# Third layer of a four-layer image model: the gates of each tap spread over the channels by transfers from DRAM, the products taken from SBUF over two chunks at a time, one copy of the values

## The chip, the cores and the metric

The kernel runs on one core of a Trainium2 chip. The metric is the device time of one execution in microseconds (us). Engine names are those of the profile: PE is the matmul engine and PEld its weight loads, DVE is VectorE, ACT is ScalarE, POOL is GpSimd, SP is the engine whose queue issues the transfers. All arithmetic spoken of here is f32.

## The reference, cut to what matters

Four layers work on an image batch of 4 x 64 x 64 pixels with 128 channels. The first two are selective scans in four directions, the fourth is a 7x7 neighbourhood attention. Only the third layer is changed. For each pixel and each of its nine neighbours (a tap) it computes two small perceptrons on the pixel and the neighbour, makes a gate of them, and averages the neighbours' values by these gates:

```
norm   = ln(tokens)                                   # 128 channels
edge   = [center, neigh, center - neigh, rel_pos]     # per pixel and tap, 9 taps
drive  = gelu(edge @ d_w1 + d_b1) @ d_w2 + d_b2       # one number per pixel and tap
resist = gelu(edge @ r_w1 + r_b1) @ r_w2 + r_b2
gate   = sigmoid(clip(lam * drive / (softplus(resist) + gamma + eps)) + bias)
values = neigh @ v_w + v_b                            # 128 channels
message = sum_taps(gate * values) / sum_taps(gate)
out    = ln(tokens + message @ o_w + o_b)
```

The gate is one number per pixel and tap, the values have 128 channels, so each gate has to reach all 128 channels before it can be multiplied.

## The kernel before

Channels lie on the 128 partitions, pixels on the free axis. An image of 4096 pixels is 8 chunks of T = 512 pixels (8 rows of 64), and the third layer works by halves of an image: four chunks. `layer2` runs over four images `b` and two halves `s`, eight halves in all, and writes out by hand the order in which work is issued; each engine takes its instructions in that order, and semaphores do the rest.

One half has two parts. `edges(b, s, side)` makes 18 steps (two perceptrons, nine taps each). A step adds the neighbours' projections (`near`, in SBUF) to the centre's (`cen`, in PSUM) with two DVE additions of 128x1024 (L1277), applies Gelu in two ACT instructions (L1282), and sums over channels with four small matmuls into `out` (L1253). Five buffers hold `hid`. Between the steps it issues pieces of the list `side`, evenly spread over the 18 steps. Then comes the fill: `gates` turns `out` into the gates `g` in five pieces (`one` to `five`, mostly DVE), and a few pieces of the next half are put between them. In `g` row 32*j + t holds tap t of chunk j.

The pieces of `side` belong to neighbouring halves:

- `finish` of the half before the last: per chunk a scaling on POOL (L1405), an ACT instruction, and a store to DRAM (L1410).
- `gather` of the last half: 18 gate pieces and then four output pieces per chunk. A gate piece is one tap of one pair of chunks: PE multiplies the rows of `g` with a 0/1 matrix `pick` so that the gate appears on all 128 partitions in PSUM (L1361), DVE multiplies it with the shifted values (L1367), one 128x512 instruction for each chunk, and POOL adds the product to `acc` (L1371), one for each chunk. The output pieces load the tokens (`xo`), apply the output weights, and take the variance (L1382 to L1388, L1209).
- `statistics` of the next image: per chunk a load on SP (`xs`, two buffers, L1191), a centring matmul (L1195) with an ACT copy, a square on POOL (L1200), a variance matmul (L1209) with an ACT copy.
- `project`: per chunk a scaling on POOL (L1219), then three matmuls (L1223) with an ACT write each (L1229): two into `near`, the third into the values `vals`, which are kept twice, for even and odd images.

The matmuls of all these pieces share two PSUM banks (`bank()`, tag mm). Every transfer is issued by SP in program order, so a transfer that waits holds the ones behind it. After the last half `layer2` runs `finish` and `gather` once more with nothing beside them; this is called the tail below. Before the first half it prepares the first image (the start-up).

The order of one gather, whose two loops the change turns round, is

```
out = [begin] + [lambda t=t, pair=pair: gate(t, pair) for pair in range(2) for t in range(NB)]
```

Of the kernel before, what the change touches and what calls it, by code (L numbers as in the profile page):

```python
# [9 lines left out]
F32 = mybir.dt.float32  # L10
# [7 lines left out]
P = 128  # L18
# [18 lines left out]
def image(t):  # L37
    return t.rearrange("p (r w) -> p r w", w=HW)
# [1034 lines left out]
class Edges:  # L1073
# [9 lines left out]
    def __init__(self, tc, C, es, nb, x_in, x_out, d_w, d_rel, d_v):  # L1083
# [2 lines left out]
        wp = es.enter_context(tc.tile_pool(name="l2w", bufs=1))  # L1086
        self.pool = es.enter_context(tc.tile_pool(name="l2k", bufs=1))
        self.psum = es.enter_context(tc.tile_pool(name="l2p", bufs=1, space=PSUM))

        w = wp.tile([P, d_w.shape[1]], F32, name="w")  # L1090
        nc.sync.dma_start(out=w, in_=d_w)
# [51 lines left out]
        nc.vector.tensor_copy(fold, C.ident[:, 0:32])  # L1143
        for j in range(1, 4):
            nc.vector.tensor_add(fold, fold, C.ident[:, 32 * j : 32 * j + 32])
        self.pick = wp.tile([P, NB, P], F32, name="pick")
        nc.vector.tensor_copy(self.pick, fold[:, 0:NB].unsqueeze(2).to_broadcast([P, NB, P]))
        row = wp.tile([P, 1], F32, name="row")
        nc.vector.reduce_sum(row, fold[:, 0:NB], axis=AX.X)
        self.mass = wp.tile([P, P], F32, name="mass")  # L1150
# [14 lines left out]


        self.near = [[wp.tile([P, HR, PW], F32, name=f"near{m}{s}") for s in range(2)] for m in range(2)]
        self.vals = [[wp.tile([P, HR, PW], F32, name=f"vals{i}{s}") for s in range(2)] for i in range(min(nb, 2))]
        for tiles in self.near:
            for t in tiles:  # L1170
                nc.gpsimd.memset(t, 0.0)
        for tiles in self.vals:
            for t in tiles:
                nc.vector.tensor_copy(t.rearrange("p h w -> p (h w)"), vb.to_broadcast([P, HR * PW]))
        self.norm = [wp.tile([P, NCH, T], F32, name=f"norm{i}") for i in range(min(nb, 2))]
        self.rstd = wp.tile([P, NCH, T], F32, name="rstd")

# [34 lines left out]
    def project(self, b, c):  # L1212

        nc = self.nc
        n = self.norm[b % 2][:, c, :]
        s, r = divmod(c, 4)

        def scale():
            nc.gpsimd.tensor_mul(n, n, self.rstd[:, c, :])  # L1219

        def part(i):
            ps = self.bank()
            nc.tensor.matmul(ps, self.vw if i == 2 else self.wnei[:, i, :], n, start=True, stop=True)  # L1223
            tiles = self.vals[b % 2] if i == 2 else self.near[i]
            bias = self.inb[:, i : i + 1]

            def rows(s, first, some):
                to = tiles[s][:, first : first + some.shape[1], 1 : 1 + HW]
                nc.scalar.activation(to, some, AF.Identity, bias=bias)  # L1229

            rows(s, 1 + r * ROWS, image(ps))


            if c == 3 and i == 2:
                rows(1, 0, image(ps)[:, ROWS - 1 : ROWS, :])
            if c == 4:
                rows(0, HR - 1, image(ps)[:, 0:1, :])

        return [scale] + [lambda i=i: part(i) for i in range(3)]

    def edge_row(self):
        for first, second in self.near:
# [50 lines left out]
    def gates(self, out, logs, half):  # L1293


        nc = self.nc
        drive, res = out

        def one():
            g = half["g"] = self.tile("g", 2)  # L1300
            d = half["drive"] = self.tile("drive")
            nc.vector.tensor_scalar_add(d, drive, self.db2)
            nc.vector.tensor_scalar_add(g, res, self.rb2)
            e = half["e"] = self.tile("inv", 2)
            nc.vector.tensor_scalar_min(e, g, 30.0)
            nc.scalar.activation(e, e, AF.Exp)

        def two():
            g, e = half["g"], half["e"]
            nc.scalar.preload_act_table_set("natural_log_exp_and_others")  # L1310
            nc.scalar.activation(e, e, AF.Ln, bias=1.0)
            self.roots(logs)
            nc.vector.tensor_max(g, g, e)
            nc.vector.tensor_scalar_add(g, g, self.gsp)
            nc.vector.reciprocal(g, g)

        def three():
            g = half["g"]
            nc.vector.tensor_mul(g, half["drive"], g)
            nc.vector.tensor_scalar(g, g, self.lam, 3.0, ALU.mult, ALU.min)  # L1320
            nc.vector.tensor_scalar(g, g, -3.0, self.ebias, ALU.max, ALU.add)
            nc.scalar.activation(g, g, AF.Exp, scale=-1.0)

        def four():
            g = half["g"]
            nc.vector.tensor_scalar_add(g, g, 1.0)
            nc.vector.reciprocal(g, g)

        def five():
            g = half["g"]  # L1330
            ps = self.bank()
            nc.tensor.matmul(ps, self.mass, g, start=True, stop=True)
            inv = self.tile("inv", 2)
            nc.vector.tensor_scalar_max(inv, ps, 1e-6)
            nc.vector.reciprocal(inv, inv)
            nc.vector.tensor_mul(g, g, inv)

        return [one, two, three, four, five]

# [6 lines left out]
    def gather(self, b, s, half):  # L1346

        nc, C = self.nc, self.C

        def begin():  # L1350
            half["acc"] = self.tile("acc", 1, (P, 4, T))
            half["var"] = self.tile("var", 1, (P, 4, T))

        def gate(t, pair):
            dy, dx = divmod(t, 3)
            js = (2 * pair, 2 * pair + 1)
            gates = []
            for j in js:
                ps = self.bank()
                part = slice(32 * j, 32 * j + 32)  # L1360
                nc.tensor.matmul(ps, self.pick[part, t, :], half["g"][part, :], start=True, stop=True)  # L1361
                gates.append(ps)
            for j, ps in zip(js, gates):
                acc = half["acc"][:, j, :]
                part = acc if t == 0 else self.tile("part", 3)
                row = j * ROWS + dy
                nc.vector.tensor_mul(  # L1367
                    image(part), image(ps), self.vals[b % 2][s][:, row : row + ROWS, dx : dx + HW]
                )
                if t:  # L1370
                    nc.gpsimd.tensor_add(acc, acc, part)  # L1371

        def output(j):
            at = {}

            def load():
                at["x"] = self.tile("xo", 2)
                nc.sync.dma_start(out=at["x"], in_=self.x_in[b, :, chunk(4 * s + j)])

            def center():  # L1380
                ps = self.bank()
                nc.tensor.matmul(ps, C.cen128, at["x"], start=True, stop=False)  # L1382
                nc.tensor.matmul(ps, self.ow, half["acc"][:, j, :], start=False, stop=True)
                nc.scalar.activation(half["acc"][:, j, :], ps, AF.Identity, bias=self.obc)

            def square():
                at["sq"] = self.tile("sqo")
                nc.gpsimd.tensor_mul(at["sq"], half["acc"][:, j, :], half["acc"][:, j, :])  # L1388

            def variance():  # L1390
                self.variance(at["sq"], half["var"][:, j, :])

            return [load, center, square, variance]

        out = [begin] + [lambda t=t, pair=pair: gate(t, pair) for pair in range(2) for t in range(NB)]
        for j in range(4):
            out += output(j)
        return out
# [22 lines left out]
def layer2(tc, C, nb, x_in, x_out, d_w, d_rel, d_v):  # L1421
    with ExitStack() as es:
# [12 lines left out]
        with tc.manual_schedule():  # L1435
# [6 lines left out]
            for b in range(nb):  # L1442
                for s in range(2):
                    side = E.finish(*before) if before else []
                    if last:
                        side = side + E.gather(*last)
                    if s == 0:
                        ahead = merged(each(E.project, b, range(6, 8)), each(E.statistics, b + 1, range(2, 6)))
                    else:
                        ahead = merged(each(E.project, b + 1, range(2, 4)), each(E.statistics, b + 1, range(7, 8)))  # L1450
                    out = E.edges(b, s, merged(side, ahead))
                    logs = [last[2]["var"]] if last else []
                    if b + 1 < nb:
                        logs.append(E.rstd[:, 0:6, :] if s == 0 else E.rstd[:, 6:8, :])
                    before, last = last, (b, s, {})
                    gates = E.gates(out, logs, last[2])
                    run(gates[:2])
                    if s == 0:
                        fill = each(E.statistics, b + 1, [6]) + each(E.project, b + 1, range(2))
                    else:  # L1460
                        fill = each(E.project, b + 1, range(4, 6)) + each(E.statistics, b + 2, range(2))
                        if b + 1 < nb:
                            fill.insert(4, E.edge_row)
                    run(merged(gates[2:], fill))
# [370 lines left out]
```

## Time and profile before

| | |
|---|---|
| median of 3 runs | 14693.77 us (14692.58 to 14696.81) |
| profiled execution, its own time | 14702.13 us |
| its span | 14700.3 us |
| third layer | 12157 to 13348 us, 1191 us of the span |
| in these 1191 us busy: PE / DVE / ACT / POOL | 912 / 661 / 584 / 467 us |
| the first two layers | up to 12157 us, DVE at 90% or more in nearly every slice |
| the fourth layer | from 13348 us, PE at 90% or more in its last three slices |

The busy times of the third layer are the sums of the view of stages. A row of a group of instructions gives line, engine, operation, output and inputs, shapes and count, then busy time and mean duration, then the idle time of the engine just before them and what ended it. PE's busy time counts a matmul until its modelled end, and an f32 matmul shows as two records.

### The profile page before, as it was taken

To read this page: it belongs to the slowest core of one execution; us is meant where nothing else is said; L and a number is where in the kernel's file an instruction comes from. 1 tells how busy PE (TensorE), PEld (TensorE's weight loads), DVE (VectorE), ACT (ScalarE), POOL (GpSimd) and SP (SyncE) were. 2 spreads that over 40 slices of the span, in tenths; PEclk is the share of its full clock that TensorE was granted. 3 is DMA by queue.
4 is the path that set the end of the run, shared out by engine and by line. 5 is a ranking of instruction groups with operands and counts; after the bars stand their busy time and mean duration, and the time that the engine had idled before them with its cause. 6 is when DMAs were issued, how large, how long until landed. Compare 5 with 4: busy or idle time off the path is not lost. (4 is left out here: it accounts for less than half of the span.)

```text
span 14700.3 us, 125581 instructions
## 1 busy us (share of the span) xinstructions
PE 10730.8 (73%) x36776; PEld 2755.0 (19%) x36776; DVE 12416.1 (84%) x10627; ACT 7877.7 (54%) x9279; POOL 9851.6 (67%) x4742
## 2 busy tenths in 40 slices
PE   5777777777776677777767767777776657777999
PEld 1111111111111111111111111111111112223555
DVE  1999999999999999999999999999999904565666
ACT  3645466555656565566555555555555335543555
POOL 1877788777888788788778888888888713441000
PEclk7676676766667666667667776667766568777999
DMA  4888888888888988988888777787787600002000
GB/s 113 220 207 218 204 216 222 216 214 217 216 224 215 224 208 208 230 217 211 216 213 213 199 195 200 197 208 200 196 205 193 166 30 24 20 18 48 13 14 8
DMA packets 853732, 2490.00 MB, mean 169 GB/s; under 512 B 143031, under 2 KB 164287, under 8 KB 844855
## 3 DMA queue, kind: packets, MB, share of 16 engines
q1 hardware_dynamic: 853047, 2481.97, 67.1%
q8 instruction: 295, 4.83, 0.1%
q14 instruction: 390, 3.19, 0.1%
HBM read 2060.21 MB, written 270.27 MB: 159 GB/s over the span
## 5 line engine op out<-in xcount | busy, mean ns | idle before, releaser
L398 POOL TENSOR_TENSOR dbu<-dub,repB 128x1024 f32<-128x1024 f32 x3072 | 7189.7, 2354 | 1511.2 <-DVE da L418 882.7
L418 DVE TENSOR_TENSOR_SCAN da<-da,state,dbu 128x1024 f32<-128x1024 f32 x2304 | 5415.4, 2350 | 297.3 <-ACT da L408 246.7
L408 ACT ACTIVATE da<-da,av 128x1024 f32<-128x1024 f32 x3072 | 3343.2, 1089 | 3647.8 <-PE da L406 3582.6
L406 PE MATMUL da<-dp,spread 96*128 96x512 bf16 x6144 | 2592.8, 516 | 2982.7 <-DVE hc L430 2959.1
L430 DVE TENSOR_TENSOR hc<-da,repC 128x1024 f32<-128x1024 f32 x3072 | 3741.0, 1218 | 40.5 <-PE ms L98 0.5
L453 PE MATMUL yps<-hc,gather 128*32 128x512 f32 x12288 | 2363.5, 852 | 2.3 <-DVE hc L430 2.3
L418 DVE TENSOR_TENSOR_SCAN da<-da,dbu 128x1024 f32<-128x1024 f32 x768 | 1759.2, 2291 | 400.7 <-POOL dbu L398 321.5
L406 PEld LDWEIGHTS <-spread 96*128 96x128 bf16 x6144 | 477.5, 107 | 6516.1 <-DVE hc L430 4124.8
L98 PE MATMUL ms<-d,wts 128*128 128x512 f32 (+3 forms) x960 | 782.0, 941 | 203.6 <-POOL d L98 140.7
L98 ACT ACT_TABLE_LOAD x640 | 821.1, 1283 | 126.8 <-DMA xcd<-o 90.8
L98 POOL TENSOR_TENSOR delta<-delta,low 128x1024 f32<-128x1024 f32 x192 | 452.3, 2356 | 529.9 <-ACT low L98 529.9
L98 PE MATMUL mp<-xd,dtw 8*128 8x512 f32 (+1 forms) x768 | 668.9, 965 | 28.7 <-DMA xd<-xdd 17.1
L98 ACT CAST parts<-delta 128x1024 bf16<-128x1024 f32 x384 | 400.5, 1043 | 295.8 <-POOL delta L98 278.3
L1371 POOL TENSOR_TENSOR acc<-acc,part 128x512 f32<-128x512 f32 x256 | 318.8, 1268 | 338.1 <-DVE part L1367 338.0
L446 PE MATMUL yps<-y,ident 128*128 128x512 f32 x576 | 520.3, 998 | 3.2 <-ACT y L471 3.2
L453 PEld LDWEIGHTS yps<-hc,gather 128*32 128x32 f32 x12288 | 283.9, 128 | 1190.3 <-issue 1184.5
L98 POOL TENSOR_TENSOR low<-delta,xc 128x1024 f32<-128x1024 f32 x192 | 501.1, 2610 | 1.7
L1615 ACT ACTIVATE s<-s,nmax 128x512 f32<-128x512 f32 x512 | 366.8, 718 | 248.7 <-DVE nmax L1612 243.9
L1282 ACT ACTIVATE hid<-hid,relb 128x1024 f32<-128x1024 f32 x288 | 320.3, 1145 | 323.0 <-DVE hid L1277 320.3
L98 ACT ACTIVATE low<-mp,av 128x512 f32<-128x512 f32 x384 | 264.1, 688 | 399.9 <-PE mp L98 397.7
L1277 DVE TENSOR_TENSOR hid<-cen,near 128x1024 f32<-128x1024 f32 x288 | 336.2, 1218 | 163.6 <-PE cen L1270 113.6
L98 PE MATMUL ms<-pad,diag 96*32 96x504 f32 (+1 forms) x2304 | 420.4, 824 | 64.0 <-ACT o L98 47.9
(230 smaller groups left out, 11780.3 us busy)
## 6 DMA issues: line engine op xcount, KB each, us to landing
dub<-dud SPq DMA_DIRECT2D x3072, 512.0 KB
dp<-parts SPq DMA_DIRECT2D x2304, 64.0 KB
repB<-xdd SPq DMA_DIRECT2D x192, 512.0 KB
repC<-xdd SPq DMA_DIRECT2D x192, 512.0 KB
dud<-low SPq DMA_DIRECT2D x192, 512.0 KB
pad<-xid SPq DMA_DIRECT2D x192, 256.0 KB
szd<-o SPq DMA_DIRECT2D x96, 256.0 KB
xcd<-o SPq DMA_DIRECT2D x96, 256.0 KB
```

What stands on the lines that cost most here:

```text
L98: return call(*args, **kw)
L398: self.nc.gpsimd.tensor_mul(dbu, self.live.pop(("dub", u)), t.prepared[step]["B"])
L406: self.nc.tensor.matmul(da[:, cols], self.C.spread[:, jj, :], dp[:, j, cols], start=True, stop=True)
L408: self.nc.scalar.activation(da, da, AF.Exp, scale=t.W.a[:, at : at + 1])
L418: nc.vector.tensor_tensor_scan(da[:, way], da[:, way], dbu[:, way], 0.0 if step % NSTEP == 0 else t.states[step - 1][:, g : g + 1], ALU.mu ...
L430: nc.vector.tensor_mul(hc, da, t.prepared[step]["C"])
L446: self.nc.tensor.matmul(out, lhs, self.view(rhs, k, c, i, HALVES), start=True, stop=False)
L453: self.nc.tensor.matmul(self.live["yps"][32 * j : 32 * j + 32, cols], self.C.gather[:, jj, :], self.live["hc", v][:, cols], start=False, s ...
L1277: nc.vector.tensor_add(hid.rearrange("p i (r w) -> p (i r) w", w=HW), cen[pair].rearrange("p i (r w) -> p (i r) w", w=HW), self.near[m][s] ...
L1282: nc.scalar.activation(hid, hid, AF.Gelu, bias=self.relb[:, m, t : t + 1])
L1371: nc.gpsimd.tensor_add(acc, acc, part)
L1615: nc.scalar.activation(s[:, i, :], s[:, i, :], AF.Exp, bias=nmax[:, h : h + 1], accum_out=total[:, h : h + 1],)
```

## The change

The gate pieces use PE no longer. After `five` the half's gates `g` (128 x 512) are stored to a DRAM tile `gd`. In the gather a new function `load(t)` fills a tile `spread` of 128 x 4 x 512 with one transfer: for tap t the four rows 32*j + t of `gd`, each read by all 128 partitions (first step of the source address 0). That is 1 MB in 512 runs of 2 KB. There are two such tiles; `load(0)` is a piece of its own ahead of the gates, and `load(t + 1)` is issued in the first piece of tap t. A gate piece is then one DVE product of 128x1024 (two chunks) with both inputs in SBUF, and one POOL addition of 128x1024. The two pairs of chunks are taken tap by tap. `pick` is gone.

The values are kept once, not for two images: `project` makes two matmuls per chunk, and the values of a half are made by five pieces (`values`: four chunks and one edge row) within the same half's `edges`. The start-up no longer makes any. The statistics of chunk 5 move from the first to the second half, and with them the ranges of the `rstd` roots.

```diff
@@ Edges.__init__
+        self.dram = es.enter_context(tc.tile_pool(name="l2d", bufs=1, space=DRAM))
-        self.pick = wp.tile([P, NB, P], F32, name="pick")
-        nc.vector.tensor_copy(self.pick, fold[:, 0:NB].unsqueeze(2).to_broadcast([P, NB, P]))
-        self.vals = [[wp.tile([P, HR, PW], F32, name=f"vals{i}{s}") for s in range(2)] for i in range(min(nb, 2))]
+        self.vals = [wp.tile([P, HR, PW], F32, name=f"vals{s}") for s in range(2)]
@@ project
-            nc.tensor.matmul(ps, self.vw if i == 2 else self.wnei[:, i, :], n, start=True, stop=True)
...
+            nc.tensor.matmul(ps, self.wnei[:, i, :], n, start=True, stop=True)
+            self.rows(self.near[i][s], 1 + r * ROWS, image(ps), i)
...
-        return [scale] + [lambda i=i: part(i) for i in range(3)]
+        return [scale] + [lambda i=i: part(i) for i in range(2)]
+    def rows(self, pad, first, some, i):
+        to = pad[:, first : first + some.shape[1], 1 : 1 + HW]
+        self.nc.scalar.activation(to, some, AF.Identity, bias=self.inb[:, i : i + 1])
+
+    def values(self, b, s):
+        def part(c, rows, first):
+            ps = self.bank()
+            n = self.norm[b % 2][:, c, rows.start * HW : rows.stop * HW]
+            ps = ps[:, 0 : n.shape[1]]
+            self.nc.tensor.matmul(ps, self.vw, n, start=True, stop=True)
+            self.rows(self.vals[s], first, image(ps), 2)
+        pieces = [lambda r=r: part(4 * s + r, slice(0, ROWS), 1 + r * ROWS) for r in range(4)]
+        edge = (4, slice(0, 1), HR - 1) if s == 0 else (3, slice(ROWS - 1, ROWS), 0)
+        return pieces + [lambda: part(*edge)]
@@ gates, piece five
             nc.vector.tensor_mul(g, g, inv)
+            half["gd"] = self.dram.tile([P, T], F32, name="gd", tag="gd", bufs=2)
+            nc.sync.dma_start(out=half["gd"], in_=g)
@@ gather
+        spread = {}
+        def load(t):
+            gd = half["gd"]
+            spread[t] = self.tile("spread", 2, (P, 4, T))
+            src = bass.AP(gd.tensor, gd.offset + t * T, [[0, P], [32 * T, 4], [1, T]])
+            nc.sync.dma_start(out=spread[t], in_=src)
         def gate(t, pair):
+            if pair == 0 and t + 1 < NB:
+                load(t + 1)
             dy, dx = divmod(t, 3)
-            js = (2 * pair, 2 * pair + 1)
-            gates = []
-            for j in js:
-                ps = self.bank()
-                part = slice(32 * j, 32 * j + 32)
-                nc.tensor.matmul(ps, self.pick[part, t, :], half["g"][part, :], start=True, stop=True)
-                gates.append(ps)
-            for j, ps in zip(js, gates):
-                acc = half["acc"][:, j, :]
-                part = acc if t == 0 else self.tile("part", 3)
-                row = j * ROWS + dy
-                nc.vector.tensor_mul(
-                    image(part), image(ps), self.vals[b % 2][s][:, row : row + ROWS, dx : dx + HW]
-                )
-                if t:
-                    nc.gpsimd.tensor_add(acc, acc, part)
+            js = slice(2 * pair, 2 * pair + 2)
+            acc = half["acc"][:, js, :]
+            part = acc if t == 0 else self.tile("part", 2, (P, 2, T))
+            row = 2 * pair * ROWS + dy
+            nc.vector.tensor_mul(
+                part.rearrange("p i (r w) -> p (i r) w", w=HW),
+                spread[t][:, js, :].rearrange("p i (r w) -> p (i r) w", w=HW),
+                self.vals[s][:, row : row + 2 * ROWS, dx : dx + HW],
+            )
+            if t:
+                nc.gpsimd.tensor_add(acc, acc, part)
...
-        out = [begin] + [lambda t=t, pair=pair: gate(t, pair) for pair in range(2) for t in range(NB)]
+        out = [begin, lambda: load(0)] + [lambda t=t, pair=pair: gate(t, pair) for t in range(NB) for pair in range(2)]
@@ layer2
                     if s == 0:
-                        ahead = merged(each(E.project, b, range(6, 8)), each(E.statistics, b + 1, range(2, 6)))
+                        ahead = merged(each(E.project, b, range(6, 8)), each(E.statistics, b + 1, range(2, 5)))
                     else:
-                        ahead = merged(each(E.project, b + 1, range(2, 4)), each(E.statistics, b + 1, range(7, 8)))
+                        ahead = merged(each(E.project, b + 1, range(2, 4)), each(E.statistics, b + 1, (5, 7)))
+                    ahead = merged(E.values(b, s), ahead)
...
-                        logs.append(E.rstd[:, 0:6, :] if s == 0 else E.rstd[:, 6:8, :])
+                        logs.append(E.rstd[:, 0:5, :] if s == 0 else E.rstd[:, 5:8, :])
```

More of the change, by code (lines that the diff above doesn't have):

```diff
@@ L1171, in __init__ @@
                 nc.gpsimd.memset(t, 0.0)
-        for tiles in self.vals:
-            for t in tiles:
-                nc.vector.tensor_copy(t.rearrange("p h w -> p (h w)"), vb.to_broadcast([P, HR * PW]))
+        for t in self.vals:
+            nc.vector.tensor_copy(t.rearrange("p h w -> p (h w)"), vb.to_broadcast([P, HR * PW]))
         self.norm = [wp.tile([P, NCH, T], F32, name=f"norm{i}") for i in range(min(nb, 2))]
@@ L1222, in part @@
             ps = self.bank()
-            nc.tensor.matmul(ps, self.vw if i == 2 else self.wnei[:, i, :], n, start=True, stop=True)
[L1224 to L1235, printed above, removed]
-            if c == 4:
-                rows(0, HR - 1, image(ps)[:, 0:1, :])
-        return [scale] + [lambda i=i: part(i) for i in range(3)]
+            nc.tensor.matmul(ps, self.wnei[:, i, :], n, start=True, stop=True)
+            self.rows(self.near[i][s], 1 + r * ROWS, image(ps), i)
+            if c == 4:
+                self.rows(self.near[i][0], HR - 1, image(ps)[:, 0:1, :], i)
+        return [scale] + [lambda i=i: part(i) for i in range(2)]
[12 more added lines that the diff above has]
+        return pieces + [lambda: part(*edge)]
     def edge_row(self):
```

## The prediction

> **What bounds the kernel now.** I read the page first, then the view of stages to find the third layer, then its groups of instructions, the order of time in one gather, and last the few rows that price what the change adds. The change touches only the 1191 us from 12157 to 13348 us; the rest of the span stays.
>
> ```profile
> span 14700.3 us, 125581 instructions
> 12581.00:12721.00 140.00, 110.63 (x294) 31.00 (x293) 82.42 (x87) 70.30 (x83) 52.94 (x44) 0.77 0.07 21
> 12594.00:12667.00 73.00, 62.10 (x150) 17.12 (x150) 41.99 (x53) 21.23 (x21) 40.27 (x33) 0.65 0.03 8
> 13260.00:13314.00 54.00, 50.09 (x75) 17.97 (x75) 24.32 (x36) 0.00 (x0) 39.07 (x32) 0.50 0.00 0
> ```
>
> The columns after the length are PE, PEld, DVE, ACT and POOL, then the granted PE clock and the DMA share. The first stage is half 3 (counted from 0), the second the gather in it, the third the tail. In both gathers PE is busiest (62 of 73 us, 50 of 54), at a clock of 0.65 and 0.50; DMA does nothing.
>
> ```profile
> L1371 POOL TENSOR_TENSOR acc<-acc,part 128x512 f32<-128x512 f32 x256 | 318.8, 1268 | 338.1 <-DVE part L1367 338.0
> L1361 PE MATMUL mm<-g,pick 32*128 32x512 f32 x576 | 315.0, 955 | 57.1 <-DVE part L1367 45.8 <-DVE acc L1367 5.9 <-DVE g L1336 5.0
> L1367 DVE TENSOR_TENSOR part<-mm,vals 128x512 f32<-128x512 f32 x256 | 168.4, 688 | 183.7 <-PE mm L1361 180.6 <-POOL acc L1371 2.5 <-issue 0.3
> L1277 DVE TENSOR_TENSOR hid<-cen,near 128x1024 f32<-128x1024 f32 x288 | 336.2, 1218 | 163.6 <-PE cen L1270 113.6 <-PE out L1253 48.7 <-ACT hid L1282 1.2
> ```
>
> DVE waits 181 us for the spread gates, PE in turn for DVE to free its two banks. In the order of time this ring takes 2.9 us a piece:
>
> ```profile
> 12611.12 1.29 DVE L1367 TENSOR_TENSOR part<-mm,vals 128x512 f32<-128x512 f32 x2 [1.64 <-PE mm L1361]
> 12611.87 2.67 PE L1361 MATMUL mm<-g,pick 32*128 32x512 f32 x4 [0.26 <-DVE part L1367]
> 12614.04 1.29 DVE L1367 TENSOR_TENSOR part<-mm,vals 128x512 f32<-128x512 f32 x2 [1.63 <-PE mm L1361]
> ```
>
> With a step's hid additions between, a tap of four chunks takes 72.1 / 9 = 8.0 us in half 3 (first product 12594.7, last product's end 12666.8).
>
> **What takes the ring's place.** A gate piece becomes one DVE product and one POOL addition of 128x1024. Alone they cost 1.22 us (L1277's shape) and 2.35 us (the page's L398, 2354 ns). But the product now reads two SBUF tiles, where L1367 and L1277 read one from PSUM. L1277 never exceeds 1227 ns, whatever POOL does. Few instructions of before have two SBUF inputs; these do:
>
> ```profile
> 13118.65 1.26 POOL L1405 TENSOR_TENSOR acc<-acc,var 128x512 f32<-128x512 f32 x1 [10.01 <-ACT var L1344]
> 13119.40 1.05 DVE L1319 TENSOR_TENSOR g<-drive,g 128x512 f32<-128x512 f32 x1
> 13118.65 2.93 POOL L1405 TENSOR_TENSOR acc<-acc,var 128x512 f32<-128x512 f32 x2 [10.01 <-ACT var L1344]
> ```
>
> L1319 takes 0.69 us in its other runs. Beside POOL it takes 1.05, and two POOL instructions take 2.93 us where 2 x 1.24 = 2.48 are usual: DVE waits until POOL's first instruction ends, then POOL's second waits. Two POOL and one DVE instruction in series would be 2.48 + 0.69 = 3.17, so 0.24 us is all that overlaps. A piece therefore costs 2.35 + 1.22 - 0.24 = 3.33 us, a tap 6.7 us; the hid additions, with one SBUF input, go beside POOL.
>
> The Trainium skill, page "SBUF — State Buffer", section "Who interferes with whom", speaks against this change: a DVE instruction with two SBUF inputs contends with a GpSimd one that reads SBUF, and the later one blocks until the first is through. The rows agree on the blocking, and show it short of complete by 0.24 us. By the page a piece is 3.57 us, a tap 7.1, and the sum below some 20 us longer.
>
> **The loads.** The nearest row is `dub`, 512 KB in 4 KB runs, each row of DRAM read by 16 partitions:
>
> ```profile
> 312.86 7.64 SPq L393 DMA_DIRECT2D dub<-dud  x5
> 317.62 4.64 POOL L398 TENSOR_TENSOR dbu<-dub,repB 128x1024 f32<-128x1024 f32 x2 [11.04 <-DMA dub<-dud]
> DMA packets 1271, 4.66 MB, mean 233 GB/s; under 512 B 133, under 2 KB 133, under 8 KB 1271
> DMA packets 384, 1.42 MB, mean 355 GB/s; under 512 B 38, under 2 KB 38, under 8 KB 384
> ```
>
> Issue to first reader is 4.8 us for 512 KB. The third line is back-to-back dub traffic alone, the fourth loads and a store of rows read once: shared rows cost a third or more of the rate. For `spread`, a row is read 128 times. I take dub's rate: 1 MB is 4.5 us of data and 4.8 + 2.25 = 7.0 us from issue to use. Bounds: 355 GB/s (3.0 us) and half of 233 (9.0 us), since sharing rises eightfold and no row shows that. A load is issued when the tap before the last has been multiplied; a tap holds its tile about 5.9 us (two products, a wait for POOL, some hid additions), so two tiles give (5.9 + 7.0) / 2 = 6.5 us a tap. With 6.7 for the port and each late at times for the other's sake I take 7.0.
>
> **The seven gathers beside edges.** SP issues `load(0)` behind the four stores of `finish`. In half 3 the last of their ACT instructions starts 9.5 us after the first hid addition, in halves 2 and 4 at 13; in the new order I put the issue at 12. It lands at 19, the second at 23.5, eight taps of 7.0 follow, the last additions take 2: the end is at 81.5. Before, the last products of halves 1 to 7 end at 76.3, 87.8, 85.3, 87.6, 86.6, 81.5 and 74.2 after the first hid addition. Half 1 has no stores in the way: `load(0)` lands near 10, end 72. Sum: 72 - 76.3 + 6 x 81.5 - 503.0 = **-18 us**. The output pieces and the last steps follow as before; PE's 315 us of L1361 go, but only where the port and the loads come next.
>
> **The rest.** Start-up: 18 projections take 21.3 us (12203.1 to 12224.4), 1.18 each; six fewer, **-7**; the five value pieces enter half 0, +1. Elsewhere they move from fills and edges to edges only: halves with s = 1 gain five ACT instructions of about 0.65 us net, half of them outside the gather, where ACT sets the pace of steps: **+4** over four halves.
>
> Fills: a value matmul stood ahead of the `mass` matmul (L1332) on PE; three fills with s = 0 lose one, 1.1 us each, the one of half 5 two: -5. In halves 1 and 3 a new wait eats this. The store of `gd` waits on SP for piece five, and behind it is queued the second `xs` load of the next image. Before, that load went out at 12395.8, forty us early; now it goes after five's product, about 12437, lands 3.2 us later (the first `xs` load: issued 12157.1, used 12160.3), and its centring, square and variance stand on PE ahead of the next `cen`. The first hid addition, at 12441.2 before, comes near 12446: +4.8 each, +9.6. Together **+4.5**. Elsewhere what queues on SP behind a waiting load (`xs`, `xo`) is needed a step or more later; I cost it at nothing, and at one landing, 3 us a half, if that cover is gone.
>
> Tail: the product of five ends at 13259.6; store 3.2, load 7.0, second load 4.5, eight taps of 6.7 and the last addition: 13330 against 13314.7 now, **+15**. Removed weights and constants lie before 12157 under other work.
>
> Sum: -18 - 7 + 1 + 4 + 4.5 + 15 = -0.5 us on 14702.1, the profiled execution's own time. That lies 8.4 us above the median, so I predict 14693.8 - 0.5, rounded to **14694 us: no change** that a measurement can tell (about 0.2%, 29 us). Its own range is 14640 to 14750: the page's 7.1, `xs` waits, 0.5 us a tap either way (28 us).
>
> **Rivals.**
>
> Slower: reading one row 128 times is slower than dub. From about 6 us of data per load (175 GB/s) the loads set the pace. At 9 us: `load(0)` lands at 23.5, nine taps end near 100 instead of 81.5, 7 x 18.5 = 130, and the tail +22 more: +165 with the remainder, 14860 us. At 7 us (150 GB/s) +65. For it: both kinds of shared load are slow, and the four rows of a tap are only 8 KB. Against: `repB`, whose rows are shared by 8, shows no better rate than `dub` with 16.
>
> Faster: the port is shared better than L1319 shows, as POOL and DVE may fall into step behind the hid additions. Then a tap costs 4.7 us of POOL, the loads 5.3 ((3.6 + 7.0) / 2): 1.7 us less on 56 taps and 14 in the tail, -109, 14585 us. Against: POOL's next instruction was seen to wait each time.
>
> That the change does not do what it says I leave out: the diff removes every L1361.
>
> **Chances.** No change 0.5, slower rival 0.33, faster rival 0.17. Within the first, a quarter falls beyond 29 us on either side. Faster: 0.13 + 0.17 = 0.30; same: 0.24 + 0.03 of weak slow cases = 0.27; slower: 0.13 + 0.30 = 0.43. The range, 14590 to 14850, leaves out half of the faster and some of the slower rival.
>
> **What would show it.** No L1361; products of 128x1024 at 1.2 us alone and up to 3 beside POOL, POOL's additions above 2.35; taps of 7 us. If products wait for `DMA spread<-gd` at nearly every tap, the slower rival holds; if they last 1.2 to 1.4 us and POOL stays at 2.35, the faster one. Wrong altogether if the span changes outside 12157 to 13348, or if the start of halves 2 and 4 is not later behind the `gd` store.

## The result and the profile after

The changed kernel takes 14689.25 us (median of 12 runs, 14672.99 to 14713.66), the kernel before 14693.17 us (12 runs beside it, 14680.32 to 14705.59). The ratio is 0.9998, with a 95% interval of 0.9989 to 1.0007: no change, as predicted. The prediction's own chances gave this outcome 0.27, and "slower" 0.43. That the total stayed doesn't show that its terms were right, so the layer is measured by itself.

"The layer" below runs in the trace from the issue of the first `xs` load to the memset that opens the fourth layer. It is a much finer measure than the whole time: two profiled executions of the kernel before give 1190.8 and 1190.6 us, while single whole runs of it lie up to 35 us apart (14671.31 to 14706.73 us in 20 runs on one chip). After the change it is 1182.0 us. A half is measured from its first hid addition to that of the next half, halves numbered 0 to 7.

The views of stages of the kernel after, with the columns as before: half 3, the gather in it (first product to last), and the products of the tail.

```profile
span 14683.7 us, 123946 instructions
12559.80:12707.20 147.40, 82.07 (x227) 21.96 (x226) 90.94 (x69) 71.81 (x83) 61.64 (x32) 0.75 0.37 89
12585.80:12644.50 58.70, 26.47 (x70) 5.74 (x70) 48.31 (x33) 17.59 (x18) 44.70 (x17) 0.65 0.67 153
13247.90:13305.40 57.50, 4.12 (x4) 1.00 (x4) 34.08 (x18) 0.18 (x1) 44.33 (x16) 0.50 0.57 155
```

PE is out of the gather (26 us instead of 62, 4 instead of 50 in the tail). DVE and POOL have taken over: 48.3 + 44.7 us in 58.7, and the DMA engines go from nothing to two thirds. The gather is 14 us shorter than before (58.7 for 73), but the half is 7 us longer (147.4 for 140.2). The groups of the layer, busy time and mean ns, then the idle time ahead of them and what ended it:

```profile
L1385 POOL TENSOR_TENSOR acc<-acc,part 128x1024 f32<-128x1024 f32 x128 | 346.0, 2718 | 285.1 <-DVE part L1379 189.1 <-ACT hid L1289 96.0
L1284 DVE TENSOR_TENSOR hid<-cen,near 128x1024 f32<-128x1024 f32 x288 | 335.1, 1214 | 163.7 <-PE cen L1277 101.7 <-PE out L1260 57.6 <-ACT hid L1289 3.3
L1379 DVE TENSOR_TENSOR part<-spread,vals 128x1024 f32<-128x1024 f32 x128 | 252.9, 2005 | 75.1 <-POOL acc L1385 40.1 <-DMA spread<-gd 34.9
L1379 DVE TENSOR_TENSOR acc<-spread,vals 128x1024 f32<-128x1024 f32 x16 | 18.9, 1222 | 66.8 <-DMA spread<-gd 66.8
L1193 PE MATMUL mm<-xs,cen 128*128 128x512 f32 x64 | 42.4, 751 | 35.3 <-DMA xs<-x 35.3
```

The third and fourth rows are the same instruction. Where no POOL addition is near (tap 0, the fourth row) it takes 1222 ns; beside the additions the mean is 2005. The hid additions, one input in PSUM, keep 1214. Most waiting for `spread` is at the first products of the eight gathers (66.8 us of 101.7). The last row shows a wait that grew unasked: the centring matmul waits 35.3 us for `xs`, 9.5 before the change. In order of time, the tail shows two taps' start and then the steady ring:

```profile
13239.26 35.15 SPq L1369 DMA_DIRECT2D spread<-gd  x7
13247.91 2.36 DVE L1379 TENSOR_TENSOR acc<-spread,vals 128x1024 f32<-128x1024 f32 x2 [13.40 <-DMA spread<-gd]
13251.53 2.36 DVE L1379 TENSOR_TENSOR part<-spread,vals 128x1024 f32<-128x1024 f32 x2 [1.26 <-DMA spread<-gd]
...
13262.83 4.48 DVE L1379 TENSOR_TENSOR part<-spread,vals 128x1024 f32<-128x1024 f32 x2 [2.23 <-POOL acc L1385]
13266.25 5.55 POOL L1385 TENSOR_TENSOR acc<-acc,part 128x1024 f32<-128x1024 f32 x2 [1.16 <-DVE part L1379]
13269.54 4.48 DVE L1379 TENSOR_TENSOR part<-spread,vals 128x1024 f32<-128x1024 f32 x2 [2.23 <-POOL acc L1385]
```

Two products take 4.48 us and two additions 5.55 (1.22 and 2.35 each when alone), DVE waits 2.23 for POOL and POOL 1.16 for DVE, and a tap lasts 13269.54 - 13262.83 = 6.71 us. This blocking of a product with two SBUF inputs and an addition is called the port below.

### The profile page after: what moved, and what is told of

Read it like the earlier page. It is cut to its first block, busy times and chain, and to the rows that moved or that the text cites. A ratio compares the mean times of both kernels' runs of the same rounds, so it can differ in the third digit from the quotient of the medians.

```text
span 14683.7 us, 123946 instructions
## 1 busy us (share of the span) xinstructions
PE 10474.2 (71%) x36216; PEld 2659.3 (18%) x36216; DVE 12490.2 (85%) x10480; ACT 7868.5 (54%) x9279; POOL 9884.3 (67%) x4614
## 3 DMA queue, kind: packets, MB, share of 16 engines
q1 hardware_dynamic: 892215, 2559.57, 69.4%
## 5 line engine op out<-in xcount | busy, mean ns | idle before, releaser
L408 ACT ACTIVATE da<-da,av 128x1024 f32<-128x1024 f32 x3072 | 3341.3, 1088 | 3661.5 <-PE da L406 3601.3
L1385 POOL TENSOR_TENSOR acc<-acc,part 128x1024 f32<-128x1024 f32 x128 | 346.0, 2718 | 285.1 <-DVE part L1379 189.1
L1284 DVE TENSOR_TENSOR hid<-cen,near 128x1024 f32<-128x1024 f32 x288 | 335.1, 1214 | 163.7 <-PE cen L1277 101.7
```

The costliest lines, as they stand in the source:

```text
L408: self.nc.scalar.activation(da, da, AF.Exp, scale=t.W.a[:, at : at + 1])
L1284: nc.vector.tensor_add(hid.rearrange("p i (r w) -> p (i r) w", w=HW), cen[pair].rearrange("p i (r w) -> p (i r) w", w=HW), self.near[m][s] ...
```

## The experiments

Each kernel starts from the one named. Whole times are given where a kernel was run several times; e1 to e4 and e11 were run once, and there the layer of that one run, against 1182.0 us after and 1190.8 before, carries the verdict.

**What sets the pace: the port or the loads.** e1 leaves the additions of taps 1 to 8 out, e2 the loads of taps 1 to 8.

```
e1:  -            if t:
     -                nc.gpsimd.tensor_add(acc, acc, part)
e2:  +            if t:
     +                spread[t] = spread[0]
     +                return
```

> Left out: POOL's additions of taps 1 to 8 to acc, so acc holds tap 0 alone; products, loads and all else stay. The port theory (a DVE product with two SBUF inputs and a POOL addition go one after the other, which sets the changed kernel's 6.7 us a tap in the tail): every product falls to 1.22 us, none lasts 3.3; what is left is the loads, (2.4 + 7.8) / 2 = 5.1 us a tap in the tail, and the third layer shrinks from 1182 us by 60 to 100. The load theory (two tiles and 7.8 us from issue to use set the pace already): products get shorter, the taps stay above 6 us, the layer loses under 25 us.

> Left out: the loads of taps 1 to 8; every tap is multiplied by the gates of tap 0. Port theory: the tail's taps stay at 6.7 us; of the 102 us that DVE waits for loads the 67 us at the first taps stay and up to 35 us go, so the layer shrinks by at most 35 us. Load theory: the taps fall to POOL's own 4.7 us, 2 us less on 64 taps, and the layer shrinks by 100 us or more.

Without the additions the layer takes 1100.5 us, 81.4 less; without the loads 1181.7, 0.3 less. Two rows of the groups, e1 first:

```profile
L1379 DVE TENSOR_TENSOR part<-spread,vals 128x1024 f32<-128x1024 f32 x128 | 152.7, 1223 | 103.9 <-DMA spread<-gd 103.9
```

```profile
L1382 DVE TENSOR_TENSOR part<-spread,vals 128x1024 f32<-128x1024 f32 x128 | 266.3, 2111 | 55.8 <-POOL acc L1388 55.8
```

In e1 a product takes 1223 ns again and the loads end its waits; a tap of the tail takes 5.3 us. In e2 the waits for loads are gone from taps 1 to 8, yet products are as long as before, and a tap still takes 6.7 us. So DVE and POOL blocking each other sets the pace in the tail. The loads stand close behind.

**Does reading a row 128 times cost?** e3 loads a block of the same size in which every partition reads rows of its own (the layer's input instead of the gates; the products are then not those of the gates).

```
-            src = bass.AP(gd.tensor, gd.offset + t * T, [[0, P], [32 * T, 4], [1, T]])
+            src = self.x_in[b].rearrange("p (j two w) -> p j two w", two=2, w=T)[:, :, t % 2, :]
```

> Changed: each load brings 1 MB of the layer's input in the same runs of 2 KB, every run read by one partition, in place of rows read by all 128 (the products are then not with gates). If reading one row 128 times slows the loads: the second load follows the first sooner than the 3.6 us seen in the tail (2.7 us at 390 GB/s), DVE's 35 us of waits for loads after the first taps mostly go, and the layer shrinks by 20 to 35 us. If sharing costs nothing at this load: the layer stays within 5 us of 1182, and issue to use in the tail stays near 7.8 us.

The layer takes 1161.7 us, 20.3 less, the lower edge of what was expected if sharing costs rate. But the taps keep their 6.7 us. What moves is the start: the first product comes some 3 us earlier in a half (20.4 after the first hid addition instead of 23.1 in half 2, 23.4 instead of 26.0 in half 3). Part of that may be that this load need not wait until the gates have landed. Loads 0 and 1 land 2.5 us apart instead of 3.6, so sharing costs about 1.1 us a megabyte, which the ring of products and additions hides.

**The store of the gates in SP's queue.** e4 sends `gd` after the last piece of the fill, so that the second `xs` load isn't behind it.

```
-            nc.sync.dma_start(out=half["gd"], in_=g)
+            half["send"] = lambda: nc.sync.dma_start(out=half["gd"], in_=g)
...
                     run(merged(gates[2:], fill))
+                    last[2]["send"]()
```

> Changed: the store of the gates to DRAM is issued after the fill's last piece, so it no longer stands in SP's queue ahead of the second load of the next image's statistics. The queue theory: in halves 2 and 4 the first addition no longer waits 11.7 us for PE behind that load but about 2.4 as before the change; the layer shrinks by 18 to 20 us, to about 1163. Rival (the wait only comes to light, since the fill itself got shorter and PE or ACT is next): under 6 us.

The layer takes 1165.8 us, 16.2 less, where 18 to 20 were expected. Half 1 goes from 127.1 to 117.9 us and half 3 from 147.4 to 137.7; half 2 gets 2.3 longer, the other halves stay within 0.2. The wait that goes is this one, of the kernel after:

```profile
12416.04 0.32 SPq L1345 DMA_DIRECT2D gd<-g  x1
12416.45 0.38 SPq L1189 DMA_DIRECT2D xs<-x  x1
12419.42 2.04 PE L1193 MATMUL mm<-xs,cen 128*128 128x512 f32 x2 [6.24 <-DMA xs<-x]
12427.73 1.23 DVE L1284 TENSOR_TENSOR hid<-cen,near 128x1024 f32<-128x1024 f32 x1 [11.72 <-PE cen L1277]
```

**The values alone.** e6 is the kernel before with one part of the change: the values are made once, in `edges`, and the order of the statistics that goes with it. The gates still reach the channels by matmuls.

```
-        self.vals = [[wp.tile(...) for s in range(2)] for i in range(min(nb, 2))]
+        self.vals = [wp.tile(...) for s in range(2)]
...
+                    ahead = merged(E.values(b, s), ahead)
```

> The kernel before, with one part of the change alone: the values are made once, before the fills, in the place that the change gives them; gates are still spread by matmuls on PE, and products and additions keep their shape of 128x512. Theory (the prediction's terms for this part): start-up 6 to 7 us shorter, half 0 about 1 longer, ACT in halves with s = 1 +1 each, fills -5 in all: the layer goes from 1191 us to about 1184 (1178 to 1190), so most of the 8.8 us that the whole change took from the layer is this part, and the new gather by itself is worth nothing. Rival: the shorter fills are worth more than the prediction gave them (2 us each and more), the layer is at 1165 to 1178, and the new gather by itself costs time, 5 to 15 us.

Both were wrong: 14712.89 us, ratio 1.0011 (1.0002 to 1.0020), and a layer of 1210.8 us, 20.0 longer than before (half 0 and the start-up together 8 shorter, halves 1 to 7 28.4 longer). e11, the kernel before again, was run to see whether that could be scatter:

> The kernel before once more, to see how far the layer of one and the same kernel moves from one profiled execution to the next. If the layer lies within 5 us of 1191, the layer's length is a finer measure than the whole time, and e6's 1211 us is a real loss in the layer; if it moves by 10 us or more, e6's loss is known from its timed runs alone.

Its layer is 1190.6 us, so the 20 us are real, and the new gather, put on top of e6, is worth 1210.8 - 1182.0 = 29 us. (The other order, the new gather with the values of before, was not run, so how the 8.8 us divide between the two parts is known in this order only.) The stage of half 6, kernel before and e6 (the PE column is the first after the length):

```profile
13001.00:13135.00 134.00, 102.61 (x274) 29.15 (x273) 83.63 (x87) 60.70 (x63) 51.02 (x41) 0.71 0.05 16
```

```profile
13007.00:13151.00 144.00, 109.97 (x281) 30.19 (x280) 83.57 (x86) 62.19 (x66) 50.90 (x41) 0.69 0.04 15
```

PE has 7.4 us more work (7 more records; an f32 matmul shows as two), and the half is 10 us longer. In halves 6 and 7 there is no next image whose statistics could have moved, and both get longer all the same (by 10.3 and 8.5 us, half 7 up to `five`'s product), so it is the values and not the moved statistics that cost time there. With the old gather PE is the busiest engine while the steps run; an image makes ten value matmuls there instead of four, while the fills lose four. The stretch from the first to the last hid addition grows by 39.4 us over halves 1 to 7, and what follows it shrinks by 11.0. Whether it is PE's work or the two banks that these pieces share was not separated.

**Starting the gather earlier.** e5 is e4 with the loads of taps 0 and 1 ahead of the stores of `finish`.

```
-        out = [begin, lambda: load(0)] + [...]
+        out = [lambda: load(0), lambda: load(1), begin] + [...]
...
+                        last_gather = E.gather(*last)
+                        side = last_gather[:2] + side + last_gather[2:]
```

> The kernel of e4 (the store of the gates issued last in the fill), and the loads of taps 0 and 1 issued first in the side work of the next half, ahead of the stores of finish on SP; taps 2 to 8 as before. Theory: what is left of the gather's late start is the queue: load 0 stands behind stores that wait for ACT until some 12 us, and the first product comes 20 to 26 us after the first hid addition. With the loads ahead, DVE's own order puts the first product at 13 to 16 us, so each of seven halves gets 6 to 9 us shorter and the layer goes from 1166 us to about 1115 (1105 to 1125); the pace of 6.7 us a tap stays. Rival 1: the start isn't what ends a half (the output pieces or POOL's scaling do); the layer stays within 10 us of 1166. Rival 2: load 0 waits for its own store of the gates, which now lies at the very end of the fill: the first product moves by less than 4 us, layer 1140 to 1166.

14651.01 us, ratio 0.9970 (0.9959 to 0.9982); layer 1149.3 us, 16.5 below e4 where 50 were expected. That lies in the range of rival 2, but not for its reason: loads now go out at most 2 us after the first hid addition, yet the first product of halves 2 to 7 still comes at 18 to 21, and it is not the load that it waits for last. The chain ahead of it, in half 3 of e5:

```profile
12540.73 0.92 SPq L1369 DMA_DIRECT2D spread<-gd  x2
...
12555.02 0.81 ACT L1423 ACTIVATE o<-acc,v 128x512 f32<-128x512 f32 x1 [6.73 <-DMA x<-o]
12559.13 1.23 DVE L1379 TENSOR_TENSOR acc<-spread,vals 128x1024 f32<-128x1024 f32 x1 [9.12 <-ACT o L1423]
```

The product writes the only `acc` tile, which ACT must first read for the stores of the older half, and ACT waits for one of two `o` tiles, whose store now goes out beside the early loads (ACT waits 49.5 us for such stores in the layer, 13.8 in the kernel after). e8 removes both at once: two `acc` tiles, and no `o`.

```
-            half["acc"] = self.tile("acc", 1, (P, 4, T))
+            half["acc"] = self.tile("acc", 2, (P, 4, T))
...
-            o = self.tile("o", 2)
-            nc.scalar.activation(o, half["acc"][:, j, :], ...)
+            o = half["acc"][:, j, :]
+            nc.scalar.activation(o, o, ...)
```

> The kernel of e5, with two acc tiles instead of one, and the last ACT instruction of finish writing into acc itself, from where it is stored: the o tiles go, which also makes the room. In e5 the first product still came 20 us after the first hid addition; its row there names ACT's write of o (L1423), which reads the one acc that the product overwrites, and which itself waits 6.7 us for an earlier store of o that runs beside the loads. Theory: that wait is the last thing ahead of the gather. Loads issued at 2 us land at 10 to 12, the first product comes at 12 to 14 in halves 2 to 7 (6 to 8 us earlier), in the tail at 11 to 13 after five instead of 17.6: the layer goes from 1149 us to about 1103 (1093 to 1115). Rival 1: DVE's order of steps places the first product near 16 anyway, half the gain: 1118 to 1130. Rival 2: the pace of the side work ends the halves, not the gather: 1138 or more.

14646.66 us, ratio 0.9955 (0.9943 to 0.9968); layer 1127.0, where the theory had 1093 to 1115. The first product comes at 11.3 to 11.6 in halves 3, 5, 6 and 7, somewhat earlier than the theory says, but at 19.0 and 18.5 in halves 2 and 4. An early start is not yet an early end: in halves 3 and 5 the last product ends at 80.0 and 77.1, as in e5 (80.2 and 77.1). In half 2 another wait is last:

```profile
12432.50 0.50 SPq L1189 DMA_DIRECT2D xs<-x  x1
...
12438.35 2.08 PE L1193 MATMUL mm<-xs,cen 128*128 128x512 f32 x2 [5.92 <-DMA xs<-x]
```

`xs` goes out behind the two megabytes of early loads, and on PE its matmul stands ahead of the next step's `out` matmuls. e12 below removes this wait.

**Getting away from the port.** e7 is e5 with odd taps spread by PE into PSUM as before, so that only even taps are loaded; e9 is e5 with the additions on DVE, so that product and addition no longer sit on two engines that block each other.

```
e7:  +            if t % 2:
     +                (four matmuls into two banks, four products of 128x512)
e9:  -                nc.gpsimd.tensor_add(acc, acc, part)
     +                nc.vector.tensor_add(acc, acc, part)
```

> The kernel of e5, but odd taps (1, 3, 5, 7) get their gates from matmuls on PE into PSUM, as in the kernel before, with four products of 128x512 a tap; even taps stay with loads and products of 128x1024. POOL's additions are all 128x1024. Theory: a product with one SBUF input doesn't block POOL, so an odd tap costs two additions of POOL, 4.7 to 5.0 us, instead of 6.7, and four odd taps take 6 to 8 us off each gather and the tail: 50 to 60 us below e5 in the layer. Rival: PE, which these matmuls bring back at 4 us a tap, and the two banks set the pace of odd taps again (8.0 us a tap in the kernel before, beside hid additions): no gain over e5 in the seven halves, or up to 30 us slower, and the tail alone shorter by about 6 us.

> The kernel of e5, with the gather's additions on DVE instead of POOL, nothing else. Theory: since product and addition block each other at the port (about 3.36 us a piece), one engine that does both in series is faster: 1.22 us for the product and as much for the addition, 2.44 a piece, 4.9 us a tap. The tail has 34 such instructions, 41.5 us, instead of 59: 16 to 18 us less. In a half DVE has 85 us of hid additions, products and additions in a stretch of 95 to 98, and the loads allow about (7.8 + 3.6) / 2 = 5.7 us a tap: 6 to 12 us off each half with a gather. Layer 1149 to about 1070 (1060 to 1095). Rival: DVE becomes the bound; hid additions queue behind products that wait for loads and behind the additions, the steps get longer by what the gather gains, and only the tail is shorter: 1125 to 1145.

e7: ratio 0.9975 (0.9965 to 0.9985), layer 1151.2 us. In the tail a pair of taps takes 11.4 us instead of 13.4 (even taps start 23.4, 35.0, 46.3 and 57.6 us after five's product), as the theory says, and the tail is 7.8 us shorter. Halves 1 to 7 are 10.3 us longer together, as the rival has it; that PE and the banks are the reason was not tested. e9: 14651.01 us, 0.9963 (0.9950 to 0.9975), layer 1140.6, within the rival's range. The tail is 8.2 us shorter, the halves only 1.4 together. In the layer's groups of e9 nothing is blocked any more:

```profile
L1379 DVE TENSOR_TENSOR part<-spread,vals 128x1024 f32<-128x1024 f32 x128 | 157.4, 1230 | 21.1 <-DMA spread<-gd 20.8
L1385 DVE TENSOR_TENSOR acc<-acc,part 128x1024 f32<-128x1024 f32 x128 | 156.8, 1225 | 4.4
```

But all of it now stands in DVE's one order with the hid additions: DVE is busy 94 to 99% of each gather in halves 1 to 7, and in half 1, where the gather always started early, nine taps still take 57.5 us (55.9 in e5).

**Together.** e10 is e8 and e9; e12 is e10 with the first `xs` load of a half ahead of the early loads.

```
e12: +                    run(stats[:1])
     +                    ahead = merged(project, stats[1:])
```

> e8 and e9 together. Theory: the two gains are of different kinds (when a gather starts, and how long it lasts), so they add: 46 + 78 us off the 1149 us of e5, limited by DVE's own work: 85 us in the stretch of the steps and some 32 in the fill make 117 us a half. Start-up 70, half 0 74, seven halves of 117 to 120 less the shorter first and last, tail 80: 1035 to 1065. Rival: DVE is the bound in e9 already, so the earlier start only moves its waits: within 10 us of e9.

> The kernel of e10, with the first xs load of each half issued ahead of the loads of taps 0 and 1, so that it no longer shares the DMA engines with them. In e8 and e10 the centring matmul of that xs stands on PE about 8 us into a half and waits 5.9 and 7.1 us for it (halves 2 and 3 of e8), and behind it on PE stand the out matmuls of the steps, which ACT and DVE then wait for. Theory: this wait goes in halves 1 to 5 (6 and 7 load no xs); load 0 lands some 1 us later for it. The first product of halves 2 and 4 comes at 12 to 13 instead of 19, and the layer goes from 1117 us to about 1095 (1088 to 1104). Rival: what these halves gain in the first 20 us they lose to DVE, which is busy 98 of 127 us and works in its written order; the layer stays within 8 us of 1117.

e10: 14614.24 us, 0.9940 (0.9926 to 0.9953), layer 1116.9. The gains do add (32.4 us below e5; e8 and e9 alone give 22.3 and 8.7), at about a third of the expected size (1035 to 1065). Its tail, without blocking, runs at 5.9 us a tap, the pace of the loads (below).

e12: **14589.67 us, 0.9926 (0.9912 to 0.9940)**, the fastest version, with a layer of 1099.6 us (1088 to 1104 expected). Of the 106 us to the kernel before, run beside it, the layer makes 91; the rest lies in parts that no edit touches, which take 13495 to 13520 us in the profiled runs. The waits for `xs` fall from 33.4 us (e10) to 3.4, and the first product comes at 11.3 to 11.9 in all of halves 2 to 7, the last ends at 68.7 to 70.6. DVE is then busy 89 to 94% of the stretch of the steps in halves 1 to 7. Half 3 of e12:

```profile
12549.05 0.37 SPq L1189 DMA_DIRECT2D xs<-x  x1
12550.64 0.92 SPq L1369 DMA_DIRECT2D spread<-gd  x2
12555.43 7.08 SPq L1424 DMA_DIRECT2D x<-acc  x4
12555.74 1.12 PE L1193 MATMUL mm<-xs,cen 128*128 128x512 f32 x2
12559.84 4.47 DVE L1379 TENSOR_TENSOR acc<-spread,vals 128x1024 f32<-128x1024 f32 x2
```

## Why the prediction was right, point by point

The sum was -0.5 us; the layer went down by 8.8: start-up -6.2, half 0 -2.0, halves 1 to 7 -16.4, tail +15.8. (The rest of the span was 8 us shorter too; the change doesn't touch it, and other executions scatter as much there.) The two big signs, gathers down and tail up, were right and nearly cancel. Inside, several terms were off and made up for each other, and "no change" leaves 29 us either way, so that the total came out is in part luck.

- **The port, 6.7 us a tap: right** (6.71 in the tail), and e1 and e2 show that it sets the pace. The row that it was read from stood for two: of the eight runs of L1319 two are beside POOL and take 1.05 us, and the other six take 0.69. The page of the Trainium skill that was weighed, "SBUF — State Buffer", section "Who interferes with whom", lets the later instruction wait until the first is through, by which the prediction estimated 7.1 us; this case measures 6.71, and the row of 0.24 us of overlap in the kernel before was the better guide.
- **The start of the gather, 19 us after the first hid addition: too early.** In halves 2 to 7 the first product comes at 23.1, 26.0, 22.9, 25.3, 20.6 and 19.9, mean 23.0. SP gets to `load(0)` at 14.4 and 17.4 us in halves 2 and 3, not 12. Part of that was misread: before the change the last ACT instruction of `finish` starts at 14.5 us in halves 2 and 4 and at 10.1 in half 3; the 13 and 9.5 are those of the third. Issue to use is 7.8 us for a load that runs nearly alone (13250.30 to 13258.12 in the tail, for load 2), not 7.0, and 7.9 to 8.7 for `load(0)` in these halves.
- **7.0 us a tap beside steps: too long.** From the landing of `load(0)` to the last product the prediction has 4.5 + 8 x 7.0 = 60.5 us; halves 2 to 7 take 57.7 to 58.7. This makes up for half of the late start: the last product was to end at 79.5 and ends at 81.4 on average, the last addition was to end at 81.5 and ends at 83.8. Half 1, which has no stores in its way, ends earlier than forecast (last addition 69.4, not 72). The -18 itself set unlike things against each other, the last additions of after and the last products of before, whose additions end some 2 us later (78.4 for 76.3 in half 1); with like ends its own terms give some 14 us more of gain. (Half 4's 87.6 is 87.3 in the trace.) Measured, the seven ends sum to 27.0 us less by products and 20.9 less by additions.
- **+4 us for ACT in halves with s = 1 didn't show in the sum:** the stretch of the steps in halves 1 to 7 shrinks by 26.3 us, about as much as the gathers. By kind of half there may be a part of it: with s = 1 the steps shrink by 10.4 us and the last products come 12.4 earlier, with s = 0 by 15.9 and 14.6. Half 0 was to be 1 longer and is 2.0 shorter.
- **The queue behind the `gd` store: right mechanism, half the size.** It was priced at 4.8 us for halves 2 and 4 each. The first hid addition of half 2 waits 11.72 us where it waited 2.4 before, 9.3 more, and e4 takes 9.2 and 9.7 us off halves 1 and 3. The likely reason is that the wait also takes back what the fill itself got shorter, since `xs` alone then sets its end. Measured from the last hid addition of a half to the first of the next, halves 1 and 3 are 13 us longer together than before, the others up to 3 us shorter or longer: +9.9 in all, for the +4.5 of the sum.
- **Start-up -7 and tail +15: right** (-6.2, and +15.8 to the last addition). Inside the tail two errors cancel: the first product comes 13.4 us after `five`'s product, not 10.2, and from there to the last addition it is 57.5 us, not 60.4, because the first three taps follow each other faster than the ring.
- **The values, a net of -7 with start-up, half 0, ACT and fills: open.** Put on the kernel before, where PE is busy 85 to 89% of the steps in halves 1 to 7, the same part costs 20 us (e6), so its price depends on the kernel around it, which the prediction didn't say. In the changed kernel PE is busy 54 to 69% of the steps there, and the values may well cost little; no run has the new gather with the values of before, so their price in the sum is not shown.
- **Rivals.** Reading a row 128 times was to be slower than `dub`; two such loads issued together land 3.6 us apart, 1.05 MB / 3.6 us = 290 GB/s against 233, so the slower rival's condition is not met. (That rival's +165 does not come out of its own terms: 130 and 22 on a sum of -0.5 make 151.) The faster rival needed products of 1.2 to 1.4 us; they average 2.0. Its pace was right, its price too high: without the blocking, and without POOL's additions too, e1 gains 81.4 us of the 109 named, the loads then setting 5.3 us a tap in the tail, as the rival had it.

## What to carry to other kernels

When work moves from one engine to another pair, look for a row in which the two run side by side: product and addition nearly in series gave 6.7 us a tap, and 6.71 was measured, while their unblocked times would have said 4.7. Then ask what sets the start of a stretch and not only its pace: of the 82 us between the kernel after and e12, the queue order of three transfers (e4, e5, e12) and one single-buffered tile (e8) gave most, and each removed wait uncovered another. And price an edit in the kernel in which it will stand: the values, down for a gain of 7 us in the changed kernel, cost 20 in the kernel before.

## What the runs showed that was not expected

- DMA reads whose rows all 128 partitions share take 3.6 us a megabyte, against 2.5 with rows of their own (e3), and 4.5 that the prediction took from `dub`.
- Two tiles bound the loads by about (hold + issue to use) / 2, an estimate that two kernels bear out. With 7.8 us from issue to use, holds of 2.4 (e1) and 3.7 us (e10) give 5.1 and 5.75 us a tap; measured 5.3 and 5.9.
- A small transfer pays for large ones in flight: an `xs` load of 256 KB took 5.9 us to its use in half 2 of e8, behind two loads of 1 MB that went out 8 us earlier, against 3.2 at the layer's start. With `xs` ahead of them (e12) the waits all but go.
- In two executions of the kernel before this layer took the same time within 0.2 us, though the whole time moves by up to 35.
